# Two attention blocks on one core: two mixing subtractions of x moved behind a bank take, and the left factors of quarter products made in parts during attention

## The chip, the cores and the metric

The kernel runs on one core of one Trainium2 chip. The metric is the time of one execution on the device in microseconds (us). A core has a matrix engine (TensorE, PE in the profile), a vector engine (VectorE, DVE), an engine for activations and copies (ScalarE, ACT), a general one (GpSimd, POOL) and SyncE (SP), whose queue issues every transfer of this kernel. Each engine works through its own list of instructions in order and waits for semaphores of the others.

## The reference

Two blocks of the same form follow one another on x of shape (8, 512, 32, 32), in float32. One block, cut to what matters:

```python
xn = group_norm(x)                                   # 8 groups in block 0, 32 in block 1
qkv = einsum('oc,bcn->bon', qkv_w, xn) + qkv_b       # n = 1024 pixels, c = 512
q, k, v = split(qkv, 3)                              # 8 heads of 64 channels
attn = softmax(einsum('bhdi,bhdj->bhij', q, k) / 8)  # 1024 x 1024 for each head
out = einsum('bhij,bhdj->bhdi', attn, v)
out = einsum('oc,bcn->bon', proj_w, out) + proj_b
x = out + x
```

## The kernel before

A unit is one image in one block: 16 units, u = 0 to 15, of which 0 to 7 are block 0. Each goes through the projections q, k and v, then attention; the output projection of the unit before stands between v and attention.

Every projection is one 2 x 2 block product after Strassen and Winograd, with seven products in place of eight. Its factors are sums and differences of quarters, made beforehand ("mixing"). For x there are four differences:

```python
def mix_right(name, low, high):
    b11, b12 = low[:, :, :FD], low[:, :, FD:]
    b21, b22 = high[:, :, :FD], high[:, :, FD:]
    ...
    parts = (
        partial(sub, t1, b12, b11), partial(sub, t2, b22, t1),
        partial(sub, t4, b21, t2), partial(sub, b12, b22, b12),
    )
    return {1: b11, 2: b21, 3: b22, 4: t4, 5: t1, 6: t2, 7: b12}, parts
```

They are VectorE instructions of 128x1024. The first two (`mixing[0]`, `mixing[1]`) run during the attention before; the last two (`mixing[2:]`: t4, and b12 in place) run at the start of the unit.

The seven products use three pairs of PSUM banks. Products 2, 4 and 3 are themselves made by seven quarter products each in q and k of units 1 to 15 (`inner`). `done` is called after each step and runs the work listed under its number in `rest`:

```python
def blocks(name, left, right, tokens, c11, others, done, u3, inner=None, rests=None):
    bx, by, bz = apair[0], sbank[0], apair[1]
    ...
    products(bx, 1, True, False)
    p1 = work(accpool, "acc", "p1")
    nc.scalar.copy(p1, bx)
    done(sums)                                # 1
    products(by, 6, True, False)
    u2 = work(trpool, "tr", "u2")
    nc.vector.tensor_add(u2, by, p1)          # the take of product 6's bank: u_q in q
    done(sums)                                # 2
    rest = last_products(bx, 2, sbank[1], bz)
    c11(bx)
    add_rest(0, 0, rest)                      # GpSimd: four sums
    done(sums)
    products(by, 7, False, False)             # adds to the bank that u2 was taken from
    ...
    nc.vector.tensor_add(u3, by, p1)
    done(sums)
    products(bz, 5, True, False)
    ...
    rest = last_products(by, 4, bx, sbank[1])
    ...
    rest = last_products(bz, 3, sbank[1], bx)
    ...
```

The right factors of the quarter products of x (r2, r3, r4) are made by GpSimd at the start of each unit, in buffers of the pool `ppool`, which has four and also holds the exponentials p of attention and the residual tiles x of the output projection:

```python
INNER = (2, 3, 4)

def mix_inner(u, right):
    for k in INNER:
        b = right[k]
        ...
        t = ppool.tile([P, 4, FD2], F32, tag="p", name=f"r{k}_{u}")
        parts += [
            partial(gp.tensor_sub, t1, b12, b11), partial(gp.tensor_sub, t2, b22, t1),
            partial(gp.tensor_sub, t3, b22, b12), partial(gp.tensor_sub, t4, b21, t2),
        ]
```

r4 is made from t4. The left factors depend on the weights alone. They are made once for each block, in units 0 and 7, by 24 GpSimd instructions of 128x128, written to a tensor in DRAM by six transfers and loaded from it at the end of each unit's attention:

```python
def mix_inner_left(l, lefts):
    add, sub = nc.gpsimd.tensor_add, nc.gpsimd.tensor_sub
    for n, k in enumerate(INNER):
        t = tpool.tile([P, 2, FD], F32, tag=("o1", "o2", "o4")[n], name=f"l{k}_{l}")
        ...
        for i in range(2):
            ...
            add(s1, a21, a22)
            sub(s2, s1, a11)
            sub(a21, a11, a21)
            sub(s4, a12, s2)
            nc.sync.dma_start(inner_left[l][:, i, n], t[:, i])
```

The main loop, cut:

```python
for u in range(2 * B):
    ...
    for part in mixing[2:]:
        part()
    if u > 0:
        w.inner, parts = mix_inner(u, right)
        for part in parts:
            part()
    ...
    projections(w, rest)
    if old is not None:
        old.res = load_res(old.u)              # four residual tiles, pool of p
    if u + 1 < 2 * B:
        xn = load_xn(u + 1)
        ...
        right, mixing = mix_right(f"x_{u + 1}", xn[:, :2], xn[:, 2:])
    if u == B - 1:                             # u = 7: weights of block 1
        lefts, mixing_w = mix_weights(1, load_weights(1), nc.gpsimd)
        for part in mixing_w:
            part()
    if u in (0, B - 1):
        mix_inner_left(units[u + 1][0], lefts)
    if old is not None:
        project(old, ...)                      # stores its tiles with nc.sync.dma_start
    ...
    rest = attention(w, at_step, at_end)       # 64 steps: 8 chunks c of 8 steps t
    old = w
```

During attention VectorE sums the exponentials of each chunk (acc), then transposes and reduces the sum (tr, red). Two small transfers carry these row sums (lt) and their reciprocals (drec, rb). `at_step` also prepares the next unit: its statistics, the power of the variance (y, on GpSimd, in the second chunk; a chunk later in unit 0), its scaling and `mixing[0]` and `mixing[1]`.

Of the kernel before, what the change touches and what calls it, by code (L numbers as in the profile page):

```python
# [32 lines left out]
def fast_path(ctx, tc, x, qkv_wT, proj_wT, vecs, groups, out, flag):  # L33
# [15 lines left out]
    B, C, N = x.shape  # L49
# [10 lines left out]
    INNER = (2, 3, 4)  # L60
# [41 lines left out]
    units = [(l, b) for l in range(2) for b in range(B)]  # L102
# [15 lines left out]
    def load_xn(u):  # L118
        t = xnpool.tile([P, CC, N], F32, tag="xn", name=f"xn_{u}")
        load_x(u, [t[:, c, :] for c in range(CC)])  # L120
        return t

    def load_res(u):
        tiles = [ppool.tile([P, N], F32, tag="p", name=f"x_{u}_{c}") for c in range(CC)]
        load_x(u, tiles)
        return tiles

    def load_weights(l):

        mats = []  # L130
        src = qkv_wT[l].rearrange("(c p) o -> p c o", p=P)
        for i in range(3):
            a = wpool.tile([P, CC, C], F32, tag=f"w{i}", name=f"w{i}_{l}")
            nc.sync.dma_start(a, src[:, :, i * C : (i + 1) * C])
            mats.append(a)
        return mats

    def mix_weights(l, mats, engine, first=0):


        lefts, parts = [], []
        add, sub = engine.tensor_add, engine.tensor_sub
        for i, a in enumerate(mats, first):
            a11, a12 = a[:, :2, :FD2], a[:, 2:, :FD2]
            a21, a22 = a[:, :2, FD2:], a[:, 2:, FD2:]
            s1, s2, s4 = (
                wpool.tile([P, 2, FD2], F32, tag=f"s{k}w{i}", name=f"s{k}w{i}_{l}")
                for k in (1, 2, 4)
            )
            parts += [  # L150
                partial(add, s1, a21, a22), partial(sub, s2, s1, a11),
                partial(sub, a21, a11, a21), partial(sub, s4, a12, s2),
            ]
            lefts.append({1: a11, 2: a12, 3: s4, 4: a22, 5: s1, 6: s2, 7: a21})
        return lefts, parts
# [6 lines that stand above are left out]
        t1, t2, t4 = (  # L162
            tpool.tile([P, 2, FD], F32, tag=f"{name[0]}{k}", name=f"{name}_t{k}")
            for k in (1, 2, 4)
        )
        sub = nc.vector.tensor_sub
# [9 lines that stand above are left out]
        gp = nc.gpsimd  # L176
        factors, parts = {}, []
        for k in INNER:
            b = right[k]
            b11, b12 = b[:, 0, :FD2], b[:, 0, FD2:]  # L180
            b21, b22 = b[:, 1, :FD2], b[:, 1, FD2:]
            t = ppool.tile([P, 4, FD2], F32, tag="p", name=f"r{k}_{u}")
            t1, t2, t3, t4 = (t[:, i, :] for i in range(4))
# [4 lines that stand above are left out]
            factors[k] = {1: b11, 2: b21, 3: b22, 4: t4, 5: t1, 6: t2, 7: t3}  # L188
        return factors, parts
# [6 lines left out]

    def mix_inner_left(l, lefts):

        add, sub = nc.gpsimd.tensor_add, nc.gpsimd.tensor_sub
        for n, k in enumerate(INNER):  # L200
            t = tpool.tile([P, 2, FD], F32, tag=("o1", "o2", "o4")[n], name=f"l{k}_{l}")
            t = t.rearrange("p a b -> p (a b)")[:, : 6 * P].rearrange("p (i s o) -> p i s o", i=2, s=3)
            for i in range(2):
                left = lefts[i][k]
                a11, a12 = left[:, 0, :P], left[:, 1, :P]
                a21, a22 = left[:, 0, P:], left[:, 1, P:]
                s1, s2, s4 = (t[:, i, j, :] for j in range(3))
                add(s1, a21, a22)
                sub(s2, s1, a11)
                sub(a21, a11, a21)  # L210
                sub(s4, a12, s2)
                nc.sync.dma_start(inner_left[l][:, i, n], t[:, i])

    def load_inner_left(u):

        l, _ = units[u]
        flat = vpool.tile([P, NT, C], F32, tag="v", name=f"il_{u}").rearrange("p t o -> p (t o)")
        n = len(INNER) * 3 * P
        made = []
        for i in range(2):  # L220
            part = flat[:, i * n : (i + 1) * n].rearrange("p (k s o) -> p k s o", s=3, o=P)
            nc.sync.dma_start(part, inner_left[l][:, i])
            made.append({k: part[:, j] for j, k in enumerate(INNER)})
        return made, flat[:, NT * C - 2 * FD :].rearrange("p (a b) -> p a b", a=2)
# [551 lines left out]
    lefts, mixing_w = mix_weights(0, load_weights(0), nc.vector)  # L776
# [5 lines left out]
    right, mixing = mix_right("x_0", xn[:, :2], xn[:, 2:])  # L782
    for part in mixing[:2]:
        part()
    rest = {g: mixing_w[2 * i + 2 : 2 * i + 4] for i, g in enumerate((1, 3, 5, 8, 10))}
# [3 lines left out]
    for u in range(2 * B):  # L789
        w = Unit()  # L790
        w.u, w.right, w.lefts, w.inner = u, right, lefts, None
        w.evac_before = []
        for part in mixing[2:]:
            part()  # L794
        if u > 0:
            w.made = old.made_next
            w.inner, parts = mix_inner(u, right)
            for part in parts:
                part()  # L799
        if u == B + 1:  # L800
            rest[16] = mixing_o
        projections(w, rest)
        if old is not None:
            old.res = load_res(old.u)
        nxt = None
        if u + 1 < 2 * B:
            xn = load_xn(u + 1)
            nxt = norm_parts(u + 1, xn)
            right, mixing = mix_right(f"x_{u + 1}", xn[:, :2], xn[:, 2:])
        else:  # L810

            again = load_xn(u)
            w.res = [again[:, c, :] for c in range(CC)]
            w.wproj = load_proj(1, "w0")
        if u == B - 1:
            lefts, mixing_w = mix_weights(1, load_weights(1), nc.gpsimd)
            for part in mixing_w:
                part()
        if u in (0, B - 1):
            mix_inner_left(units[u + 1][0], lefts)  # L820

        def stats_of(*which):
            for i in which if nxt is not None else ():
                nxt[1](i // NH, i % NH)

        if old is not None:
            old.left = left_o
            stats_after = {3: (0, 1, 2), 4: (3,), 6: (4, 5), 7: (6, 7)}
            project(old, lambda g: stats_of(*stats_after.get(g, ())))
            w.evac_before = old.evac  # L830
            if old.u == B - 1:
                (left_o,), mixing_o = mix_weights(1, [load_proj(1, "wproj")], nc.vector, 3)


        late = 1 if u == 0 else 0

        def at_step(s, state):
            if nxt is None:
                return
            st, stats, aggregate, means, variances, scales, apply, _ = nxt  # L840
            c, t = divmod(s, NT)

            pair = (c + 1) % 2
            free = state["free"][pair]
            c -= late
            if u == 0 and NT // 2 <= s < NT:
                stats_of(2 * s - NT, 2 * s - NT + 1)
            if c == 1 and t == 1:
                aggregate()
            elif c == 1 and t == 3:  # L850
                means(abank[2 * pair], *free)
                free[:] = [st["last"]]
            elif c == 1 and t == 5:
                variances(abank[2 * pair], *free)
                free[:] = [st["last"]]
            elif c == 2 and t == 0:
                scales()
            elif 2 <= c < 2 + CC and t in (4, 6):
                apply(c - 2, int(t == 6))
            elif c == 2 + CC and t in (2, 5):  # L860
                mixing[int(t == 5)]()

        def at_end():
            if u + 1 < 2 * B:
                w.made_next = load_inner_left(u + 1)

        rest = attention(w, at_step, at_end)
        old = w

# [276 lines left out]
```

## Time and profile before

| | |
|---|---|
| time, median of 3 runs | 3347.62 us (3344.77 to 3348.38) |
| profiled execution, first to last instruction | 3346.6 us |
| mean granted TensorE clock | 0.997 of full speed |
| r, GpSimd, 128x256 from xn alone | 60 instructions, 1252 ns mean |
| acc, VectorE, 128x1024 | 768 instructions, 1239 ns mean |
| scores (s from q, k), TensorE | 7808 matmuls, 591 ns mean |
| first product of units 6, 7 and 8 starts at | 1235.97, 1441.59 and 1667.79 us |

In the profile a line such as `r<-xn` names the tile written and the tiles read, without their numbers; L348 is line 348 of the kernel. L348 holds whole products, L366 quarter products, L599 scores, L627 the product of attention and v, L607 the exponentials, L400 the take u2, L411 the take u3, L794 the two subtractions `mixing[2:]`, L799 the right factors r, L208 to L211 the left factors, L212 their transfers and L524 the stores of the output projection. SPq is the queue of SyncE. Matmul durations overlap, since they are pipelined; their starts tell the pace. In a timeline the columns are the start, the length of the merged run of instructions, engine, line, operation, tiles, shape and count, and in brackets the idle time of that engine before, with what ended it.

### The profile page before, as it was taken

How to read it: one execution, taken by the hardware profiler on the slowest of the kernel's cores; microseconds unless marked ns; L12 is line 12 of the kernel's file. 1: busy time of each engine (PE TensorE's matmuls, PEld its weight loads, DVE VectorE, ACT ScalarE, POOL GpSimd, SP SyncE). 2: the span in 40 equal slices, each digit the busy share in tenths (PEclk: the TensorE clock that was granted, in tenths of full speed). 3: DMA queues.
4: the chain of work that ended last, by engine and by line, in shares of the span. 5: the costliest groups of instructions: out<-in, count | busy, mean ns of one | idle time of the engine just before them, and what ended most of it. 6: DMA issues, size and time to landing. Idle time of an engine off the chain costs nothing.

```text
span 3346.6 us, 53654 instructions
## 1 busy us (share of the span) xinstructions
PE 3286.8 (98%) x21542; PEld 1738.3 (52%) x21542; DVE 2411.0 (72%) x2977; ACT 1526.2 (46%) x1909; POOL 616.9 (18%) x620
## 2 busy tenths in 40 slices
PE   8999999999999999997999999999999999999999
PEld 4445464554645546463464554645546464554633
DVE  4876948769486795855948679486795857859577
ACT  1542716436174362732716436174362734527344
POOL 1031030401204022043030401204022040210400
PEclk9999999999999999998999999999999999999999
DMA  2111110111201112012111111201112011120111
GB/s 77 48 41 70 35 64 28 53 58 35 76 21 47 58 35 82 15 47 109 35 64 42 51 57 35 76 21 47 58 35 82 15 47 64 35 76 15 53 70 47
DMA packets 72908, 169.50 MB, mean 51 GB/s; under 512 B 21456, under 2 KB 23248, under 8 KB 72656
## 3 DMA queue, kind: packets, MB, share of 16 engines
q1 hardware_dynamic: 72656, 166.01, 15.2%
q8 instruction: 175, 2.87, 0.4%
q14 instruction: 77, 0.63, 0.1%
HBM read 127.95 MB, written 36.44 MB: 49 GB/s over the span
## 4 chain that ended last, share of the span: by engine, by line
PE 84%; DVE 11%; issue 3%; POOL 1%; DMA 1%; ACT 1%; SPq 0%; DVEq 0%; POOLq 0%; ACTq 0%
PE a L627 21%; PE s L599 21%; PE a L348 18%; PE s L348 15%; DVE acc L646 6%; PE a L366 4%; PE s L366 3%; DVE tr L659 1%; PE a L599 1%; DVE x_t L794 1%; ACT p L607 1%; DVE u_q L400 1%; DVE acc L644 1%; DVE xn L794 1%; DVE red L669 0%
## 5 line engine op out<-in xcount | busy, mean ns | idle before, releaser
L607 ACT ACTIVATE p<-s 128x1024 f32<-128x1024 f32 x976 | 998.1, 1024 | 836.7 <-PE s L599 766.7
L627 PE MATMUL a<-p,v 64*64 64x512 f32 x8192 | 1100.2, 590 | 17.5 <-ACT p L607 17.4
L599 PE MATMUL s<-q,k 64*64 64x512 f32 x7808 | 1057.9, 591 | 1.6 <-DVE v L488 1.4
L646 DVE TENSOR_TENSOR acc<-acc,p 128x1024 f32<-128x1024 f32 x768 | 951.4, 1239 | 91.1 <-ACT p L607 42.7
L627 PEld LDWEIGHTS a<-p,v 64*64 64x64 f32 x8192 | 382.4, 131 | 515.6 <-ACT p L607 368.5
L599 PEld LDWEIGHTS s<-q,k 64*64 64x64 f32 x7808 | 381.3, 133 | 443.0 <-issue 440.2
L799 POOL TENSOR_TENSOR r<-xn 128x256 f32<-128x256 f32 x60 | 75.1, 1252 | 1197.9 <-DVE acc L646 1130.2
L275 POOL TENSOR_TENSOR y<-var,half 128x4 f32<-128x4 f32 x16 | 32.2, 2015 | 1004.8 <-DVE var L273 1004.8
L644 DVE TENSOR_TENSOR acc<-p,p 128x1024 f32<-128x1024 f32 x128 | 153.7, 1201 | 31.1 <-ACT p L607 31.1
L659 DVE STREAM_TRANSPOSE tr<-acc 128x1024 f32<-128x1024 f32 x128 | 157.9, 1233 | 0.0
L669 DVE TENSOR_REDUCE red<-tr 128x32 f32<-128x1024 f32 x128 | 153.8, 1202 | 0.5
L653 DVE TENSOR_TENSOR ao<-a,tmp 128x512 f32<-128x512 f32 x128 | 87.9, 687 | 69.2 <-ACT tmp L652 69.2
L348 PE MATMUL s<-xn,w 128*128 128x512 f32 x256 | 118.3, 606 | 18.0 <-DVE u_q L400 18.0
L348 PE MATMUL a<-xn,w 128*128 128x512 f32 x272 | 126.8, 610 | 4.4 <-DVE xn L303 4.4
L396 ACT COPY p_o<-a 128x1024 f32<-128x1024 f32 x15 | 15.2, 1012 | 244.2 <-PE a L348 244.2
L348 PE MATMUL a<-w,xn 128*128 128x256 f32 x512 | 115.7, 379 | 0.0
L348 PE MATMUL s<-x_t,s2w 128*128 128x512 f32 x256 | 115.1, 592 | 0.0
L348 PE MATMUL a<-x_t,s1w 128*128 128x512 f32 x256 | 115.1, 592 | 0.0
L466 POOL TENSOR_TENSOR k<-k,m_k 128x512 f32<-128x512 f32 x90 | 112.3, 1270 | 0.0
L466 POOL TENSOR_TENSOR q<-q,m_q 128x512 f32<-128x512 f32 x90 | 112.3, 1269 | 0.0
L348 PE MATMUL a<-ao,wproj_wproj 128*128 128x512 f32 x240 | 107.9, 592 | 0.0
L348 PEld LDWEIGHTS a<-w,xn 128*128 128x128 f32 x512 | 97.3, 190 | 13.7 <-issue 0.5
(195 smaller groups left out, 3768.2 us busy)
## 6 DMA issues: line engine op xcount, KB each, us to landing
rb<-drec SPq DMA_DIRECT2D x128, 256.0 KB, 3.9
xn<-mid SPq DMA_DIRECT2D x36, 512.0 KB, 4.9
il<-il SPq DMA_DIRECT2D x30, 576.0 KB, 4.3
xn<-x_dram SPq DMA_DIRECT2D x32, 512.0 KB, 5.1
x<-x_dram SPq DMA_DIRECT2D x32, 512.0 KB, 3.2
mid<-x SPq DMA_DIRECT2D x64, 256.0 KB, 2.1
x<-mid SPq DMA_DIRECT2D x28, 512.0 KB, 3.5
out_dram<-x SPq DMA_DIRECT2D x56, 256.0 KB, 2.1
```

Source lines behind the costliest of these rows:

```text
L348: nc.tensor.matmul(dst, at[:, c, ts(i, P)], moving[:, c, :], start=start and c == 0 and not (tokens and i % 2), stop=stop and c == 1, skip ...
L366: nc.tensor.matmul(dst, left[j], right[j], start=start, stop=stop, skip_group_check=True)
L466: w.last[sel].append(nc.gpsimd.tensor_add(cols, cols, rest[:, i, :]))
L599: nc.tensor.matmul(bank[e * H : (e + 1) * H, j, :], w.k[pr][j * H : (j + 1) * H, t * P + e * H : t * P + (e + 1) * H], w.q[pr][j * H : (j ...
L607: exp = nc.scalar.activation(p, bank, AF.Exp, scale=SCALE)
L627: nc.tensor.matmul(banks[r][j * H : (j + 1) * H, :], w.v[rows, t, lo : lo + D], p[rows, j, :], start=(t == 0), stop=(t == NT - 1),)
L644: nc.vector.tensor_add(acc, state["first"], p)
L646: nc.vector.tensor_add(acc, acc, p)
L653: i1 = nc.vector.tensor_add(w.ao[pr // 2][:, pr % 2, ts(qh, FD)], banks[1], tmp)
L659: nc.vector.transpose(tr, state["acc"].pop(c))
L669: nc.vector.tensor_reduce(red[:, :, qh, :], state["tr"].rearrange("p j (f i) -> p j f i", i=BL), AX.X, ALU.add)
L799: part()
```

## The change

It has two parts. The subtractions `mixing[2:]` are no longer issued at the start of the unit but under step 2 of the projection, behind the take u2, and in reversed order: first b12, which product 7 reads, then t4, which product 4 reads. The last four pieces of `mix_inner`, which make r4 from t4, go with them. The aim is that VectorE reaches the take sooner. Second, the left factors are no longer issued ahead of the output projection but in three parts (one for each of k = 2, 3, 4) at the first steps of chunks 3, 4 and 5 of attention in units 0 and 7. The aim is that neither GpSimd nor the transfer queue is taken by them ahead of the output projection.

```diff
     def mix_inner_left(l, lefts):
 
+
         add, sub = nc.gpsimd.tensor_add, nc.gpsimd.tensor_sub
-        for n, k in enumerate(INNER):
+
+        def part(n, k):
             t = tpool.tile(...)                      # (body unchanged, cut)
             ...
                 nc.sync.dma_start(inner_left[l][:, i, n], t[:, i])
+
+        return [partial(part, n, k) for n, k in enumerate(INNER)]
@@
-        for part in mixing[2:]:
-            part()
+
+        rest.setdefault(2, []).extend([mixing[3], mixing[2]])
         if u > 0:
             w.made = old.made_next
             w.inner, parts = mix_inner(u, right)
-            for part in parts:
+            for part in parts[:-4]:
                 part()
+            rest[2].extend(parts[-4:])
@@
-        if u in (0, B - 1):
-            mix_inner_left(units[u + 1][0], lefts)
+        left_parts = mix_inner_left(units[u + 1][0], lefts) if u in (0, B - 1) else ()
@@
             c, t = divmod(s, NT)
+            if t == 0 and 3 <= c < 3 + len(left_parts):
+                left_parts[c - 3]()
```

## The prediction

> **What bounds the kernel now.** I read the page first, for the share of each engine, then the waits of TensorE, then two stretches in order of time, one for each large wait.
>
> ```profile
> PE 3286.8 (98%) x21542; PEld 1738.3 (52%) x21542; DVE 2411.0 (72%) x2977; ACT 1526.2 (46%) x1909; POOL 616.9 (18%) x620
> ```
>
> TensorE works 3286.8 of 3346.6 us. The change takes no matrix product away, so it can win no more than the idle 60 us and what slow clocks after idle time cost. The waits of TensorE (waiter, releaser, total us, times, longest) say where the idle time lies:
>
> ```profile
> PE s L348 <- DVE u_q L400: 18.0, 15, 2.7
> PE a L627 <- ACT p L607: 17.4, 1, 17.4
> PE a L255 <- DVE mv L247: 11.1, 1, 11.1
> PE a L348 <- DVE xn L303: 4.4, 1, 4.4
> ```
>
> The last two are the start of the kernel (first load, first norm), which the change leaves alone. The first is the wait in product 7 of the q projection, once in each of units 1 to 15, and the second is one single hole. Both parts of the change aim at one of them.
>
> The single hole is in unit 7, at the start of its attention. The windows of attention in unit 6 (first) and unit 7 (second) show it; the columns after the stretch are its length, then the busy time of PE, PEld, DVE, ACT and POOL, the granted clock and the DMA share:
>
> ```profile
> 1331.33:1441.59 110.26, 110.26 (x1033) 49.84 (x1032) 98.99 (x123) 76.57 (x83) 3.84 (x2) 1.00 0.07 22
> 1537.22:1667.79 130.57, 112.95 (x1032) 51.14 (x1032) 99.73 (x125) 76.58 (x83) 17.38 (x29) 0.93 0.12 39
> ```
>
> The same work takes 130.57 - 110.26 = 20.31 us longer in unit 7: 17.4 us idle, and the rest a lower clock after it. The timelines of the DMA queue and of ScalarE say who holds it up:
>
> ```profile
> 1514.80 2.26 SPq L134 DMA_DIRECT2D w<-qkv_wT_dram  x3
> 1542.40 9.17 SPq L212 DMA_DIRECT2D il<-l  x6
> 1551.67 4.57 SPq L524 DMA_DIRECT2D mid<-x  x8
> ```
> ```profile
> 1556.71 1.94 ACT L607 ACTIVATE p<-s 128x1024 f32<-128x1024 f32 x2 [39.21 <-DMA mid<-x]
> ```
>
> The eight stores of the output projection (mid<-x) leave after the six transfers of the left factors (il<-l), because they stand behind them in SyncE's queue. The left factors wait for GpSimd, which first mixes the weights of layer 1 (done at 1540.6) and then makes 24 small pieces up to 1551.2. The residual tiles x share a pool of four with the exponentials p, so the first exponential waits until a store has landed, at 1556.7. In unit 6 the same stores left from 1318.5 on and the first exponential ran at 1332.49, 1.16 us after the first score product.
>
> The repeated wait, in unit 6, on VectorE and then TensorE:
>
> ```profile
> 1242.14 1.22 DVE L669 TENSOR_REDUCE red<-tr 128x32 f32<-128x1024 f32 x1
> 1243.28 1.61 DVE L794 TENSOR_TENSOR x_t<-xn,x_t 128x1024 f32<-128x1024 f32 x1
> 1244.82 1.21 DVE L794 TENSOR_TENSOR xn<-xn 128x1024 f32<-128x1024 f32 x1
> 1245.95 1.21 DVE L400 TENSOR_TENSOR u_q<-s,p_q 128x1024 f32<-128x1024 f32 x1
> ```
> ```profile
> 1239.51 3.60 PE L348 MATMUL s<-x_t,s2w 128*128 128x512 f32 x8
> ...
> 1245.53 0.59 PE L366 MATMUL s<-r,w 128*128 128x256 f32 x2
> 1247.22 3.70 PE L348 MATMUL s<-xn,w 128*128 128x512 f32 x8 [1.09 <-DVE u_q L400]
> ```
>
> Product 6 is ready at 1243.11, the reduction of the attention before ends at 1243.36, and only then come two subtractions and the take u_q. Pairs of quarter products follow each other every 0.43 us, so product 7 could start at 1245.53 + 0.43 = 1245.96; it starts at 1247.22.
>
> **What the Trainium skill says.** "SBUF — State Buffer", section "Who interferes with whom": a VectorE instruction with two SBUF inputs contends with a GpSimd instruction that reads SBUF, and the later one blocks; one with at most one SBUF input does not. The trace agrees: GpSimd's pieces r take 1.70 us against VectorE's sums and 0.73 beside its transpose and reduction, and the first subtraction takes 1.61 us where it meets the last r piece (1243.09 to 1243.82), the second 1.21. "Perfetto Trace Analysis", section "DMA Instruction — HWDGE (DVE, Sync)": the sequencer waits for the semaphores first and is free for the next instruction only when the descriptors are made. So a transfer that waits for GpSimd holds the stores behind it, as seen. "TensorE: Matmul & The Clock Gate", section "What's actually happening": an idle window of about 3.4 us halves the clock. After the 17.4 us hole the granted clock is 0.90 over 1558 to 1580.
>
> **The change part by part.**
>
> Part A, the order of the two subtractions in units 1 to 15. No instruction is added or removed. The take u_q moves ahead of both, the in-place one (b12) comes second and t4 third. Product 7 needs the bank after u_q and the new b12, so one subtraction still lies between. In unit 6: reduction to 1243.28 (start of the next), u_q (one input in PSUM, 1.21, starts follow at about 1.14) starts at 1243.28, b12 starts at 1244.42 and ends at 1245.63. By then the last piece of r3 (to 1243.82) is done and r4 has not started, because it needs t4; so b12 takes 1.21 and not 1.61. 1245.63 is 0.33 before 1245.96: the wait goes altogether. It is worth 1247.22 - 1245.96 = 1.26, and the first product after it loses its refill (start to start 3.54 in place of 3.43), 0.11: 1.37 us. Fourteen units have the same 1.09 us of idle time, so 14 x 1.37 = 19.2 us.
>
> Unit 1 is different: its VectorE runs later, product 7 starts at 217.41 where 214.53 was possible, and it then takes 5.24 us in place of 3.43 at a reduced clock. In the new order b12 ends at about 213.87 + 1.14 + 1.22 = 216.23, which saves 1.1 us, and some of the 1.8 us of the clock may go with it: 2 us.
>
> Behind it t4 is late by about 1245.6 + 1.2 - 1244.9 = 1.9 us, and so are the four pieces of r4: 1246.8 + 4 x 0.73 = 1249.7, or 1251.5 if all contend. The first product that reads them would stand at 1245.96 + 2 x 3.43 = 1252.8. They lie beside the matrix products. GpSimd's later sums into q are needed at the start of attention, some 80 us on.
>
> In unit 0 product 7 does not wait, and b12 would end at 29.7 against its start at 30.44: nothing.
>
> Part B, the left factors in unit 7. The six transfers leave the queue ahead of the stores, and the stores leave as VectorE finishes the tiles (1523 to 1539). GpSimd's mixing of weights stays where it is, and so does its contention with VectorE in the projection, which made that stretch 95.63 in place of 95.36. The last tiles are finished some 0.6 to 1.7 us later against the scores than in unit 6, so the third exponential may wait 0.5 us. Gain 20.3 - 0.5 = 19.8 us.
>
> The 24 pieces themselves, 0.46 us each alone, have nothing to wait for in the program order but GpSimd's power of the variance, so they run right after it in one go, not one part in each chunk. VectorE is busy 92% there (36.64 of 40 us between 1600 and 1640), so they are stretched, to 1.3 or 1.7 us each, 31 to 41 us. VectorE's own sums keep their pace beside GpSimd's r pieces: four in 5.19 us (1.30 each) against six in 7.87 (1.31) with GpSimd idle. I take 0.5 us for both units together.
>
> Sum: 19.2 + 2 + 19.8 - 0.5 = 40.5 us. 3347.6 - 40.5 = 3307.1 us, 1.2% less.
>
> **The rivals.**
>
> First, b12 takes the place of the take in the wait: if VectorE arrives 0.4 us later, or u_q and b12 contend with GpSimd, each unit keeps up to 0.8 us. For it: the margin is only 0.33 us. Against it: one of u_q's inputs is in PSUM, and no r piece runs under b12. Part A would then give about 10 us, and the time would be 3317.
>
> Second, the factors wait again elsewhere. Their transfers now stand before the loads lt of the row sums, which VectorE needs at the next odd chunk. In unit 0 the pieces start at about 135, where the second part must be made before the sums' loads at 156.9. At 1.3 us a piece it is done at 156.2, at 1.7 at 162; then the reciprocals, and sums behind them, are held for some 2 to 5 us. In unit 7 the norm comes a chunk earlier, so there is room. That would make 3309 to 3312.
>
> Third, unit 7 keeps a wait, for the mixed weights or for the stores, which now share the DMA with 3 MB of weights (landing to about 1527). For it: GpSimd and VectorE do contend there. Against it: the first stores to matter leave at about 1537, 10 us after. A few us; if the whole hole stayed, the time would be 3327.
>
> Fourth, the clock: with fewer pauses the granted clock might fall. It is 1.00 in every stretch with TensorE fully busy, so I give this little weight.
>
> **Range and chances.** Both parts right give 3307; the first rival takes up to 10 us back and the second up to 5, and the runs before spread by 3.6 us. On the other side unit 1's clock and the half us allowances can bring 2 or 3 more. 3302 to 3316. Faster by over 2% would need 3280.7, or 67 us, more than all idle time: 1%. Slower by over 2% would need a new stall of 107 us: 1%.
>
> **What would show it.** TensorE's wait for u_q is gone in units 2 to 15, with at most a short wait for the b12 subtraction at unit 1; the starts of units are 204.25 us apart (205.62 before). The eight stores of unit 7 leave between about 1514 and 1530 (1524 to 1539 less the 10 us saved by then), and its attention takes 110 to 111 us. The factor pieces follow the power of the variance directly. Waits of 0.3 us or more for b12 in all units would break part A; a wait of ScalarE for a store in unit 7 over 2 us would break part B; a wait of VectorE for lt in unit 0 would be the second rival.

## The result, and the profile after

| | before | after |
|---|---|---|
| median of 4 runs | 3348.0 us | 3311.32 us (3310.78 to 3311.97) |
| profiled execution | 3346.6 us | 3308.9 us |
| mean granted TensorE clock | 0.997 | 1.000 |

The ratio is 0.9892, with a 95% interval of 0.9875 to 0.9909: 36.7 us or 1.1% less, where 3307 with a range of 3302 to 3316 was predicted. The page of the changed kernel begins with the busy times:

```profile
PE 3281.0 (99%) x21542; PEld 1736.5 (52%) x21542; DVE 2435.9 (74%) x2977; ACT 1525.1 (46%) x1909; POOL 616.7 (19%) x620
```

The waits of TensorE, in full (waiter, releaser, total us, times, longest):

```profile
PE a L259 <- DVE mv L251: 11.5, 1, 11.5
PE a L352 <- DVE xn L307: 4.0, 1, 4.0
PE a L631 <- ACT p L611: 2.3, 1, 2.3
PE s L352 <- DVE xn L441: 1.6, 1, 1.6
PE s L603 <- DVE v L492: 1.4, 1, 1.4
PE a L259 <- DVE e L272: 0.9, 1, 0.9
PE a L603 <- DVE x L539: 0.2, 1, 0.2
```

The line numbers are 2 to 6 higher than before (L352 was L348, L404 was L400, L441 the two subtractions wherever they run from the list). The 18.0 us for u_q are down to one wait of 1.6 us for b12, in unit 1, and the 17.4 us for p to 2.3. But these 2.3 us are not what is left of the hole: they are a new wait, in unit 0. The three windows are the attention of units 0, 6 and 7 of the changed kernel (stretch, length, then busy PE, PEld, DVE, ACT, POOL, granted clock, DMA share, GB/s):

```profile
92.65:205.47 112.82, 110.49 (x1032) 47.73 (x1032) 102.00 (x126) 76.41 (x83) 18.27 (x26) 1.00 0.14 45
1323.91:1434.17 110.26, 110.26 (x1034) 49.82 (x1033) 99.02 (x123) 76.53 (x83) 3.83 (x2) 1.00 0.07 21
1528.42:1639.14 110.72, 110.56 (x1034) 48.82 (x1033) 101.27 (x125) 76.35 (x83) 24.95 (x29) 1.00 0.12 36
```

Unit 7 has lost its 20 us: 110.72 after 130.57. Unit 0 has gained 2.20: 112.82, where the same stretch took 110.62 before.

The queue of SyncE and ScalarE around the start of unit 7's attention:

```profile
1506.28 2.38 SPq L134 DMA_DIRECT2D w<-qkv_wT_dram  x3
1515.57 15.16 SPq L528 DMA_DIRECT2D mid<-x  x8
```
```profile
1529.60 1.99 ACT L611 ACTIVATE p<-s 128x1024 f32<-128x1024 f32 x2 [20.62 <-PE s L603]
1531.99 1.03 ACT L611 ACTIVATE p<-a 128x1024 f32<-128x1024 f32 x1 [0.40 <-DMA mid<-x]
1534.51 1.94 ACT L611 ACTIVATE p<-s 128x1024 f32<-128x1024 f32 x2 [1.49 <-DMA mid<-x]
```

The stores follow the weights directly and leave over 15 us as the tiles are finished. The first exponential waits for TensorE, as in a usual unit; the third and fourth wait 0.40 and 1.49 us for stores. TensorE loses 0.46 us against unit 6, but not by these waits (VectorE, then TensorE):

```profile
1529.12 1.26 DVE L539 TENSOR_TENSOR x<-a,u_o 128x512 f32<-128x512 f32 x2
```
```profile
1530.53 1.09 PE L603 MATMUL a<-q,k 64*64 64x512 f32 x8 [0.16 <-DVE x L539]
```

The second score product starts 2.11 us after the first (at 1528.42), where unit 6 takes 1.77: its bank is free only when VectorE has finished the last tile of the output projection. These 0.34 us are there before either wait for a store, they do not grow while those last, and 0.12 us come in two small steps later.

Now the units 1 to 15. From the first product of a unit to that of the next it is 204.51 us in most units, and 205.62 before: 1.11 us less, not the 1.37 of the prediction. Unit 6 of the changed kernel, VectorE, then TensorE, then GpSimd:

```profile
1236.96 1.22 DVE L404 TENSOR_TENSOR u_q<-s,p_q 128x1024 f32<-128x1024 f32 x1
1238.10 1.22 DVE L441 TENSOR_TENSOR xn<-xn 128x1024 f32<-128x1024 f32 x1
1239.23 1.22 DVE L441 TENSOR_TENSOR x_t<-xn,x_t 128x1024 f32<-128x1024 f32 x1
...
1244.42 0.71 DVE L690 TENSOR_TENSOR one<-red,lt 32x64 f32<-32x64 f32 x1
1245.06 1.29 DVE L693 TENSOR_TENSOR two<-lt 32x64 f32<-32x64 f32 x1
1246.38 1.19 DVE L694 TENSOR_TENSOR tot<-one,two 32x64 f32<-32x64 f32 x1
...
1248.67 1.39 DVE L461 SCALAR_TENSOR_TENSOR q<-a,vec,il 128x512 f32<-128x512 f32 x2
```
```profile
1239.64 3.60 PE L352 MATMUL s<-xn,w 128*128 128x512 f32 x8
...
1249.53 0.59 PE L370 MATMUL s<-xn,s4w 128*128 128x256 f32 x2
1250.12 0.70 PE L370 MATMUL a<-xn,s4w 128*128 128x256 f32 x2
1250.65 0.59 PE L370 MATMUL a<-xn,il 128*128 128x256 f32 x2
```
```profile
1242.84 0.73 POOL L441 TENSOR_TENSOR r<-x_t,r 128x256 f32<-128x256 f32 x1
1243.53 0.73 POOL L390 TENSOR_TENSOR m_q<-m_q 128x256 f32<-128x256 f32 x1
1244.33 0.72 POOL L391 TENSOR_TENSOR m_q<-m_q 128x256 f32<-128x256 f32 x1
1245.01 2.49 POOL L470 TENSOR_TENSOR q<-q,m_q 128x512 f32<-128x512 f32 x2
```

The take, b12 and t4 take 1.22 us each, and product 7 starts without a wait, as predicted. The loss comes later. Pairs of quarter products should follow at 0.43 us, but from 1249.53 to 1250.12 it is 0.59 and to the next 0.53. The pair at 1250.12 is quarter product 2 of product 3, which writes into the bank of product 5. That bank is free once VectorE's combination (q from a, vec, il, two instructions, which end at 1250.06) has read it, and the combination is late because the reciprocals of the last head pair stand ahead of it. In the kernel before, two and tot took 0.21 us each; here 1.29 and 1.19. The same place before, VectorE, then GpSimd:

```profile
1252.73 0.21 DVE L689 TENSOR_TENSOR two<-lt 32x64 f32<-32x64 f32 x1
```
```profile
1250.24 2.50 POOL L466 TENSOR_TENSOR q<-q,m_q 128x512 f32<-128x512 f32 x2
```

GpSimd's two sums ended at 1252.74 there. In the changed kernel they start 1.1 us later in the unit (r4, ahead of them, waits for t4), and the reciprocals start 1.4 us earlier, so that two and tot fall on them.

### The profile page after: what moved, and what is told of

The parts are those of the page before. It is cut to its first block, busy times and chain, and to the rows that moved or that the text cites. A ratio compares the mean times of both kernels' runs of the same rounds, so it can differ in the third digit from the quotient of the medians.

```text
span 3308.9 us, 53663 instructions
## 1 busy us (share of the span) xinstructions
PE 3281.0 (99%) x21542; PEld 1736.5 (52%) x21542; DVE 2435.9 (74%) x2977; ACT 1525.1 (46%) x1909; POOL 616.7 (19%) x620
## 4 chain that ended last, share of the span: by engine, by line
PE 99%; DVE 1%; DMA 0%; issue 0%; ACT 0%; POOL 0%; SPq 0%; ACTq 0%
PE a L631 26%; PE s L603 25%; PE a L352 20%; PE s L352 16%; PE a L370 4%; PE s L370 4%; PE a L603 1%; PE s L554 0%; PE a L554 0%; DMA xn<-x_dram 0%; DVE x L539 0%; DVE stats L247 0%; PE a L259 0%; ACT p L611 0%; DVE acc L648 0%
## 5 line engine op out<-in xcount | busy, mean ns | idle before, releaser
L352 PE MATMUL a<-xn,w 128*128 128x512 f32 x272 | 125.6, 605 | 4.0 <-DVE xn L307 4.0
L400 ACT COPY p_o<-a 128x1024 f32<-128x1024 f32 x15 | 15.2, 1012 | 244.2 <-PE a L352 244.2
L352 PE MATMUL s<-xn,w 128*128 128x512 f32 x256 | 115.2, 593 | 1.6 <-DVE xn L441 1.6
L352 PE MATMUL a<-w,xn 128*128 128x256 f32 x512 | 115.7, 379 | 0.0
L352 PE MATMUL a<-x_t,s1w 128*128 128x512 f32 x256 | 115.1, 592 | 0.0
L352 PE MATMUL s<-x_t,s2w 128*128 128x512 f32 x256 | 115.1, 592 | 0.0
L352 PE MATMUL a<-ao,wproj_wproj 128*128 128x512 f32 x240 | 107.9, 592 | 0.0
L352 PEld LDWEIGHTS a<-w,xn 128*128 128x128 f32 x512 | 97.3, 190 | 13.7 <-issue 0.5
```

Of the source, the lines that this page charges most:

```text
L352: nc.tensor.matmul(dst, at[:, c, ts(i, P)], moving[:, c, :], start=start and c == 0 and not (tokens and i % 2), stop=stop and c == 1, skip ...
```

## The experiments

Each kernel is compared with the kernel before in the same set of runs. Beside the median I read the start of each unit and of its attention from the timeline of TensorE, which repeats to some hundredths of a us in most units; single units differ by 0.1 to 0.3.

**One part at a time: the order of the subtractions alone.** The kernel before with this edit:

```diff
-        for part in mixing[2:]:
-            part()
+        rest.setdefault(2, []).extend([mixing[3], mixing[2]])
...
-            for part in parts:
+            for part in parts[:-4]:
                 part()
+            rest[2].extend(parts[-4:])
```

> The kernel before with only the two subtractions (and r4) moved behind the take; the left factors stay ahead of the output projection. Theory (the two parts act on separate stretches): units 2 to 15 are 204.5 us apart, unit 1 206.2, the hole of 17.4 us in unit 7 stays whole: 15.5 + 2.8 = 18 us off 3348, 3330 us. Rival (part of the gain belongs to the two together, as the later clock or the freer GpSimd): under 12 us off, over 3336.

Measured: 3328.99 us against 3346.11, ratio 0.9947 (0.9931 to 0.9964). Units lie 204.5 us apart, unit 1 takes 206.11 (before 208.95), unit 0's attention stays at 110.62 and unit 7's at 130.11. Its waits of TensorE keep the hole and lose u_q:

```profile
PE a L627 <- ACT p L607: 17.4, 1, 17.4
...
PE s L348 <- DVE xn L437: 1.6, 1, 1.6
```

**The left factors alone.** The changed kernel with the first edit taken back.

> The kernel before with only the left factors moved into attention. Theory: unit 7's attention falls from 130.6 to 110.7 us, unit 0's rises from 110.6 to 112.8 because GpSimd's pieces meet VectorE's short instructions there: 19.9 - 2.2 = 17.7 us off, 3330 us. Rival (unit 0's loss comes from the moved subtractions): unit 0 stays at 110.6 and the time is 3328.

Measured: 3329.5 us against 3346.11, ratio 0.995 (0.9933 to 0.9966). Unit 7's attention takes 110.77, unit 0's 112.82, and units lie 205.62 apart as before. So each part works on its own stretches, and unit 0's loss belongs to the left factors. By the medians the parts save 17.1 and 16.6 us, 33.7 together, where the whole change saved 36.7 in another set of runs; where these 3 us lie is not shown.

**Only the transfers of the factors moved.** The kernel before, with GpSimd's pieces in their old place:

```diff
+        sends = []
...
-                nc.sync.dma_start(inner_left[l][:, i, n], t[:, i])
+                sends.append(partial(nc.sync.dma_start, inner_left[l][:, i, n], t[:, i]))
+        return sends
...
+            if t == 0 and 3 <= c < 6 and sends:
+                for send in sends[2 * (c - 3) : 2 * (c - 2)]:
+                    send()
```

> The kernel before with GpSimd's 24 pieces in their old place, ahead of the output projection, and only their six transfers moved behind the stores (two each at chunks 3, 4, 5). Theory (the transfers, which wait in the queue ahead of the stores, make the hole; GpSimd's time does not): the hole of unit 7 goes as with the whole part, and unit 0 keeps 110.6 us: about 19.5 us off, 3328 us. Rival (GpSimd's work itself holds the projection or attention): most of the hole stays, 3340 or more.

Measured: 3328.6 us against 3346.11, ratio 0.9943 (0.9927 to 0.996). Unit 0's attention is 110.63; of unit 7's this is the window:

```profile
1537.82:1648.98 111.16, 110.70 (x1033) 54.59 (x1032) 100.93 (x125) 76.59 (x83) 27.01 (x29) 1.00 0.12 36
```

With the 24 pieces still issued ahead of the projection, 130.57 - 111.16 = 19.4 of the 20.3 us are gone. So the hole was the queue: the stores stood behind transfers that waited for GpSimd. The 0.9 us that remain are all that GpSimd's work, the late tiles and the late stores cost together. In unit 1 the projections took 1.3 us more than before (100.02 against 98.69), at a lower clock behind the wait for u_q (see the last section).

**Unit 0's factors back in their old place.** The changed kernel with:

```diff
         left_parts = mix_inner_left(units[u + 1][0], lefts) if u in (0, B - 1) else ()
+        if u == 0:
+            for part in left_parts:
+                part()
+            left_parts = ()
```

> The changed kernel with unit 0's factors back in their old place; unit 7's stay in attention. Theory (in unit 0 the pieces run just when VectorE does the short instructions of reciprocals and norm, and stretch them by 1.9 us, which empties the pool of p): the attention of unit 0 falls from 112.8 to 110.6 us, and the time by 2.2 to 3309 us. Rival (unit 0's loss is a matter of the start): no change, 3311.

Measured: 3309.38 us against 3346.11, ratio 0.9888 (0.9872 to 0.9905); unit 0's attention is 110.62 again, and the 2.3 us have left the waits. The median does not show this: it lies 36.7 us below the kernel before, as that of the changed kernel did in its own set. In the changed kernel VectorE's short instructions at the head of chunk 3 ran beside GpSimd's pieces (VectorE and GpSimd, then ScalarE and TensorE, which VectorE held up):

```profile
137.97 0.48 DVE L693 TENSOR_TENSOR two<-lt 32x64 f32<-32x64 f32 x1
138.49 0.38 DVE L694 TENSOR_TENSOR tot<-one,two 32x64 f32<-32x64 f32 x1
...
141.57 0.38 DVE L293 TENSOR_TENSOR scale<-rstd,vec 128x4 f32<-128x4 f32 x1
141.99 0.38 DVE L295 TENSOR_TENSOR ms<-mean,scale 128x4 f32<-128x4 f32 x1
```
```profile
137.92 0.46 POOL L213 TENSOR_TENSOR l<-w,l 128x128 f32<-128x128 f32 x1
...
141.90 0.45 POOL L210 TENSOR_TENSOR l<-w 128x128 f32<-128x128 f32 x1
```
```profile
144.06 1.02 ACT L611 ACTIVATE p<-s 128x1024 f32<-128x1024 f32 x1 [3.53 <-DVE acc L648]
```
```profile
145.23 1.09 PE L631 MATMUL a<-p,v 64*64 64x512 f32 x8 [2.33 <-ACT p L611]
```

In this experiment the same instructions are short, without GpSimd:

```profile
138.11 0.20 DVE L693 TENSOR_TENSOR two<-lt 32x64 f32<-32x64 f32 x1
138.34 0.21 DVE L694 TENSOR_TENSOR tot<-one,two 32x64 f32<-32x64 f32 x1
...
140.62 0.16 DVE L295 TENSOR_TENSOR ms<-mean,scale 128x4 f32<-128x4 f32 x1
```

From the first of these (one) to the next sum of exponentials it is 4.83 us in the changed kernel (137.65 to 142.48) and 2.90 here (138.00 to 140.90). Those 1.9 us empty the pool of four p tiles: ScalarE waits 3.53 us for the sum that frees one (1.33 in this experiment), and TensorE 2.33 us for ScalarE. In unit 7 of the changed kernel the same pieces cost no such wait: there they end at 1574.78, as the short instructions begin (at 1574.77), and two and tot take 0.20 and 0.21 us.

**The reciprocals one step later.** The changed kernel with:

```diff
-            4: [lambda: reciprocals(CC - 1)], 10: [divide_last],
+            5: [lambda: reciprocals(CC - 1)], 10: [divide_last],
```

> The changed kernel with the reciprocals of the last head pair moved one step on, behind the combination that frees the bank of product 5. Theory (in the changed kernel these short instructions hold the combination, and TensorE waits 0.26 us in each unit at the second quarter product of product 3): the wait goes in 14 units, 3.6 us off 3311, 3307.7 us, units 204.25 us apart. Rival (the wait comes from something else, as the copies of ScalarE or the order of banks): units stay 204.5 apart, 3311.

Measured: 3308.89 us against 3347.68, ratio 0.9884 (0.9868 to 0.9901). Most units lie 204.26 us apart, 1.36 less than before: the predicted 204.25. Unit 7 took 0.8 us more than that leads to (205.51, against 204.97 less 0.25), with a wait of TensorE of 0.6 us for a tile x of the output projection at the start of attention, which ate part of the gain in this trace.

**GpSimd's sums later instead.** The changed kernel with the reciprocals in place and GpSimd's sums for product 2 behind those for product 4:

```diff
-        rest = last_products(bx, 2, sbank[1], bz)
+        rest2 = last_products(bx, 2, sbank[1], bz)
         c11(bx)
-        add_rest(0, 0, rest)
...
         add_rest(1, 0, rest)
+        add_rest(0, 0, rest2)
```

> The changed kernel with GpSimd's four sums for product 2 in q and k put behind those for product 4; the reciprocals stay at step 4. Theory (the short instructions take long only because GpSimd works beside them: 1.29 and 1.19 us in place of 0.20): with GpSimd idle they take 0.2 each, TensorE's wait goes, 3307.7 us. Rival (the combination is late even without GpSimd, since VectorE's order is what it is): units stay 204.5 apart, 3311.

Measured: 3306.96 us against 3347.68, ratio 0.9879 (0.9862 to 0.9895); units again 204.26 us apart (unit 7: 205.20). VectorE in unit 6:

```profile
1243.88 0.20 DVE L690 TENSOR_TENSOR one<-red,lt 32x64 f32<-32x64 f32 x1
1244.01 0.21 DVE L693 TENSOR_TENSOR two<-lt 32x64 f32<-32x64 f32 x1
1244.25 0.21 DVE L694 TENSOR_TENSOR tot<-one,two 32x64 f32<-32x64 f32 x1
...
1246.25 1.41 DVE L461 SCALAR_TENSOR_TENSOR q<-a,vec,il 128x512 f32<-128x512 f32 x2 [0.62 <-PE a L352]
```

VectorE's order is that of the changed kernel and only GpSimd is out of the way: two and tot are back at 0.21, and the combination waits for TensorE instead of the other way round. The two mends touch different engines and give the same 204.26, so the wait came from the two meeting.

**b12 ahead of the take, only t4 behind it.** The changed kernel with:

```diff
-        rest.setdefault(2, []).extend([mixing[3], mixing[2]])
+        mixing[3]()
+        rest.setdefault(2, []).extend([mixing[2]])
```

> The changed kernel with the in-place subtraction b12 back at the start of the unit, ahead of the take; only t4 and r4 stay behind it. VectorE has the same work ahead of product 7 either way. Theory (b12 has two inputs in SBUF and meets the last r3 piece of GpSimd, while the take has one): b12 takes 1.6 us in place of 1.22, product 7 waits 0.2 to 0.3 us in each of 14 units: 3 to 4 us more, 3314 to 3315. Rival (order within the pair does not matter): 3311.

Measured: 3310.98 us against 3347.68, ratio 0.9891 (0.9875 to 0.9908); units 204.48 us apart. The time is the rival's, the cause is not. VectorE and TensorE in unit 6:

```profile
1237.49 1.60 DVE L798 TENSOR_TENSOR xn<-xn 128x1024 f32<-128x1024 f32 x1
1239.01 1.21 DVE L404 TENSOR_TENSOR u_q<-s,p_q 128x1024 f32<-128x1024 f32 x1
```
```profile
1239.74 0.59 PE L370 MATMUL s<-r,w 128*128 128x256 f32 x2
1240.28 3.70 PE L352 MATMUL s<-xn,w 128*128 128x512 f32 x8
...
1250.27 0.59 PE L370 MATMUL s<-xn,s4w 128*128 128x256 f32 x2
1250.70 0.59 PE L370 MATMUL a<-xn,s4w 128*128 128x256 f32 x2
```

b12 does take 1.60 us, and product 7 starts 0.54 after the last pair in place of 0.43, with the longer refill 0.22 us in all. But the pair of product 3 follows at 0.43: TensorE is later, and the combination is 0.5 us earlier in the unit than in the changed kernel (it ends at 1250.05, 0.65 before the pair), since two met a shorter sum of GpSimd, of 128x256, and took 0.75 in place of 1.29. The expected 3 to 4 us do not appear, because the first wait (0.22) comes in place of the second (0.26) and is not added to it.

**Both mends.** The changed kernel with the edits of the unit 0 and the reciprocals experiments.

> The changed kernel with both mends: unit 0's factors in their old place and the reciprocals one step on. If the two losses are what the theories say and add up: 3311.3 - 2.2 - 3.6 = 3305.5 us. If either theory is wrong: 3307.7 to 3311.

Measured: 3306.42 us against 3347.68, ratio 0.9878 (0.9862 to 0.9895). In its trace unit 0's attention is 110.63, units 2 to 14 lie 204.26 us apart but for two (204.53 and 204.46), and the span is 3303.3 us. It has the lowest median of the kernels, 4.9 us below the changed one. The two were measured in different sets of runs and their ratios' intervals overlap, so it is the stretches of the traces that show the gain; from the kernel with GpSimd's sums later (3306.96) the times do not tell it apart.

## Why the prediction was right, and where its terms were off

The total lay within the range: 36.7 us measured, 40.5 predicted. By its steps:

- **The hole of unit 7** (19.8 predicted): 130.57 - 110.72 = 19.85. That the queue made it, and not GpSimd's time, is shown by moving the transfers alone. The 0.5 us set aside for late tiles came to 0.46, but by another way: not through the third exponential, but mostly through a bank for which TensorE itself waited. The stores left from 1515.57 to 1530.7, where 1514 to 1530 was said.
- **The take ahead of both subtractions** (1.37 in each of 14 units): the product after product 7 starts 1.36 us sooner in the unit, but at the unit's end 1.11 remain. The step that failed is the one on the delayed t4 and r4, which "lie beside the matrix products", with GpSimd's later sums needed only "some 80 us on". They do lie beside the products, but the sums that they push back also lie beside VectorE's reciprocals, which I had not placed in the new order. The term was 14 x 1.11 = 15.5 in place of 19.2, and both ways of parting the two give back 1.36.
- **Unit 1** (2 predicted): 208.95 - 206.20 = 2.75. Its wait fell from 2.7 to 1.6 us and the clock stayed at 1.00, so more of the slow product 7 was saved than I took.
- **The 24 pieces** (0.5 for both units): 2.20 lost in unit 0, next to nothing in unit 7. I had read the long sums of VectorE and not the short instructions, which made the loss. The reading was wrong as well: the four sums in 5.19 us begin at 1230.16 in the kernel before, the r pieces only at 1234.16. Two sums wholly beside r pieces took 3.40 us (from 1236.95), and 2.55 with GpSimd idle (from 1222.02). Beside the smaller left factor pieces long sums did lose little: five took 6.89 us in unit 7 (from 1566.20), and 6.53 with GpSimd idle (from 1187.36 before). That the pieces run in one go after the power of the variance was right (from 134.07 in unit 0), their length was not: most took 0.46 there and not 1.3 to 1.7, while VectorE had gaps and was on its transpose and on short instructions.
- **The rivals**: the first (b12 in place of the take) holds for unit 1 alone. The second named a wait for lt in unit 0; the loss was in unit 0, but there was no such wait, since the pieces were done by 149.3. The third came as ScalarE's 1.9 us for stores, which cost TensorE nothing that the trace shows. The fourth did not occur.

The terms add up: 19.85 + 15.5 + 2.75 - 2.2 = 35.9, and of the other 1.8 of the 37.7 us between the two profiled executions 1.26 lie ahead of unit 0's attention (92.65 against 93.91, a stretch that varies from run to run, so this part is chance), and the rest in single units.

## What to carry to other kernels

A transfer that waits for a slow producer holds every later transfer of its queue: look for what stands behind it, above all stores that free buffers. When work is moved off a wait, place all that moves with it in the new order on each engine, and look at the short instructions there too: fourteen of them lost 1.9 us together in unit 0. And a gain that comes out smaller by a constant amount in each round is worth one more look at the spacing of the instructions of the busiest engine: the 0.26 us did not appear in any list of waits.

## What the runs showed of the hardware

A VectorE instruction of 32x64 that takes 0.20 us alone took 1.19 to 1.29 beside a GpSimd sum of 128x512 of 1.25, so it waited for nearly the whole of it; beside pieces of 128x128 (0.46) those of 128x4 went from 0.16 to 0.38. Long VectorE sums of 128x1024 lose too: two took 3.40 us in place of 2.55 beside r pieces, and stretched these from 0.73 to 1.70. This agrees with the blocking that "SBUF — State Buffer" describes in "Who interferes with whom".

The clock fell after a shorter pause than I expected. In unit 1 TensorE's pause of 2.7 us was followed by a product that took 5.24 us (before) and 6.57 (with the transfers moved) in place of 3.43, while after a pause of 1.6 us it took 3.54. "TensorE: Matmul & The Clock Gate" ("What's actually happening") speaks of an idle window of about 3.4 us; here 2.7 was enough. The loss differed with the same pause because the granted clock was 0.50 for 3.41 us before (217.57 to 220.98) and for 6.82 with the transfers moved (216.04 to 222.86); why the second lasted longer is not shown. After the pause of 2.33 us in unit 0 of the changed kernel it stayed at 1.00.
